# Layer 1's stack: the second feed-forward products issued together, and three score masks in one VectorE instruction

## The chip, the cores and the metric

The kernel runs on one core of a Trainium2 chip. A core has TensorE (PE in the profile; PEld is its weight load), VectorE (DVE), ScalarE (ACT), GpSimd (POOL) and SyncE (SP, which here issues DMAs). Times are device microseconds of one execution; lower is better.

## The reference

Four transformer-like layers are applied to an activation of 4 sequences x 1024 positions x 128 features, in fp32. Each layer has the same frame:

```python
h = _layernorm(x, axis=-1) * (1 + ca) + sa
x = x + ga * attn(h)
h = _layernorm(x, axis=-1) * (1 + cb) + sb
x = x + gb * ffn(h)
```

Layer 0's attention is a decaying linear attention and its feed-forward part a mixture of 8 experts. Layers 2 and 3 have chunked delta-rule attention and one expert chosen per sequence. Layer 1's attention is itself a stack of four blocks (`L = 4`, 16 heads of 8 features, feed-forward width 512), and this is where most of the change lies. One block is:

```python
q, k, v = x @ Wq + bq, x @ Wk + bk, x @ Wv + bv          # q, k through elu + 1
scores = q k^T within a chunk of 128 positions, lower triangle kept
out = (q KVcum + scores v) / (q . Kcum + sum of scores + eps)
x = _ln(x + out @ Wo + bo)
y = gelu(x @ W1 + b1) @ W2 + b2
x = _ln(x + y)
```

## The kernel before

Activations lie feature-major: 128 partitions hold the features, the free dimension holds 4 sequences x 1024 positions. One step `n` (of 8) takes a chunk of 128 positions of all four sequences, 512 columns, and a matmul result of 512 fp32 columns fills one of the eight PSUM banks.

Work within a half layer is written as Python generators ("chains") that ask for buffers (`take`, `one`), announce the time that the next instructions will take on each engine (`run`), and wait for marks (`wait`). `Flow.run` is a planner: it plays all chains against a clock of each engine, picks the chain of the lowest rank among those that can start within 0.1 us of the earliest, and so emits one fixed order of instructions. The order is then kept by the four compute engines (`in_order`). The announced lengths (`act_len`, `dve_len`, `mm_len` and numbers written out) thus never appear as instructions; they only decide what is issued ahead of what, in all four layers.

Layer 1's stack is `l1_attn`. Its chains, for 4 blocks x 8 steps:

- `prep_step` makes q, k and v. Each of q and k is a matmul into a `ps` bank, a DVE `min` into a buffer `fe` (L878) and an ACT relu (L879); ACT takes two exponentials (L888) and POOL adds them (L891). Then come the transposed keys (L903, L905), running sums of keys (L920, L923), denominators (L938, L939), and four masked copies of q (`qx`, L959).
- `scores` makes, for each sequence `b`, four score matrices at once with 32-row strips of the array, into the four banks of a "quad". There is one quad (`sp`). Its banks are written in the order 2, 3, 1, 0.
- `mask_dve` multiplies banks 0, 1, 2 by the triangle with three DVE instructions (L1010). `mask_act` copies bank 3 with ACT (L1023), and POOL masks the copy (L1026). When both are through, the quad is free.
- `values` multiplies the masked scores by v into the `acc` bank (L1085), after the carried state's share (L1071).
- `attn_out` divides, applies Wo and adds the residual (L1101, L1109).
- `tail_step`, run by two alternating chains, does the first norm, the feed-forward part (L1132 is the GELU, L1138 adds the result) and the second norm.

Banks are dealt out as follows: `ps` has three for all of `prep_step`, `state`, `attn_out` and `tail_step` and the norms, `acc` has one, the quad four. The feed-forward part before the change is

```python
po = yield from one("ps")
for f in range(4):
    u = yield from one("fu")
    pb = yield from one("ps")
    ...                                  # first product into pb, GELU into u, pb given back
    mm(po.t, W(1, "w2", 4 * l + f), flat(u.t), f == 0, f == 3)
    fl.give(u)
```

`norm` (used in all layers) transposes a step (L493), copies it out with ACT (L496), takes mean and variance with DVE (L502, L504), adds 1e-5 to the variance with DVE (L505, tile `ve`), raises to the power -0.5 with POOL (L507), scales with DVE (L510), transposes back (L518) and applies the affine part with ACT (L522 or L526). All matmuls go through the helper at L292, so the profile tells them apart by tiles.

Of the kernel before, what the change touches and what calls it, by code (L numbers as in the profile page):

```python
# [9 lines left out]
F32 = mybir.dt.float32  # L10
# [5 lines left out]
P = 128  # L16
# [218 lines left out]
def dve_len(n):  # L235
    return 0.16 + 0.00104 * n


def act_len(n):
    return 0.25 + 0.00083 * n  # L240
# [6 lines left out]
TR_LEN = 0.11  # L247


@with_exitstack  # L250
def adaln_stack_kernel(ctx: ExitStack, tc: tile.TileContext, a):
# [36 lines left out]
    def acc():  # L288
        return new(acp, [P, 512], "acc")
# [180 lines left out]
    def banks():  # L470
        return [ps() for _ in range(6)] + [acc() for _ in range(2)]
# [13 lines left out]
    def norm(fl, src, dst, affine):  # L485


        xb = yield from one("xt")
        pb = yield from one("ps")
        p = v4(pb.t)  # L490
        yield run(PE=4 * TR_LEN)
        for t in range(4):
            PE.transpose(p[:, t, :], src[:, t, :], ident)  # L493
        xt = xb.t
        yield run(ACT=act_len(512))
        S.copy(xt, p)  # L496
# [12 lines left out]
        for t in range(4):  # L509
            V.tensor_scalar(  # L510
                xt[:, t, :], xt[:, t, :], mv.t[:, t, 0:1], rs.t[:, t : t + 1], ALU.subtract, ALU.mult
            )
        fl.give(st, mv, ve, rs)
        pb = yield from one("ps")
        p = v4(pb.t)
        yield run(PE=4 * TR_LEN)
        for t in range(4):
            PE.transpose(p[:, t, :], xt[:, t, :], ident)  # L518
        fl.give(xb)
        if len(affine) == 1:  # L520
            yield run(ACT=act_len(512) + 0.1)
            S.activation(dst, p, AF.Identity, scale=affine[0][0], bias=affine[0][1])  # L522
        else:
            yield run(ACT=4 * act_len(P) + 0.4)
# [26 lines left out]
    def route(fl, n, wr, bias):  # L551


        rb, mb = (yield from one("rt")), (yield from one("rm"))
        p, oh1, oh2, rest = (rb.t[:, i, :].rearrange("p (b e) -> p b e", e=E) for i in range(4))
        m, r, s = (mb.t[:, i, :] for i in range(3))
        pb = yield from one("ps")
        lg = pb.t[:, : B * E].rearrange("p (b e) -> p b e", e=E)
        yield run(PE=4 * mm_len(E))
        for b in range(B):  # L560
            mm(lg[:, b, :], h4[:, b, n, :], wr)
        yield run(DVE=0.5)
        if bias is not None:
            V.tensor_tensor(p, lg, rep(bias, B), ALU.add)
            lg = p
        V.tensor_reduce(m, lg, AX.X, ALU.max)
        V.tensor_tensor(p if bias is None else rest, lg, spread(m, E), ALU.subtract)
        fl.give(pb)
        if bias is None:
            yield run("exp", ACT=0.3)  # L570
            S.activation(p, p, AF.Exp)
            yield run(DVE=0.6)
            normalise(p, s)
            yield run(DVE=2.0)
            first_max(p, m, oh1, r)
            V.scalar_tensor_tensor(rest, oh1, -BIG, p, ALU.mult, ALU.add)
            first_max(rest, m, oh2, r)
            V.tensor_tensor(oh1, oh1, oh2, ALU.add)
            V.tensor_tensor(p, p, oh1, ALU.mult)
        else:  # L580
            ex = yield from one("ex")
            yield run("exp", ACT=0.3)
            S.activation(ex.t, rest, AF.Exp)
            yield run(DVE=2.4)
            first_max(p, m, oh1, r)
            V.scalar_tensor_tensor(rest, oh1, -BIG, p, ALU.mult, ALU.add)
            first_max(rest, m, oh2, r)
            V.tensor_tensor(oh1, oh1, oh2, ALU.add)
            V.tensor_tensor(p, ex.t, oh1, ALU.mult)
            normalise(p, s)  # L590
            fl.give(ex)
        gt, gd = (yield from one("gt")), (yield from one("gd"))
        pb = yield from one("ps")
        yield run(PE=4 * TR_LEN)
        for b in range(B):
            PE.transpose(pb.t[:E, b * P : (b + 1) * P], p[:, b, :], ident)
        fl.give(rb, mb)
        yield run(ACT=act_len(512))
        S.copy(gt.t, pb.t[:E, :])
        fl.give(pb)  # L600
        yield run(SP=0.2)
        nc.sync.dma_start(gd.t, gt.t)
        fl.mark(("gates", n), 2.5)
        return gt, gd


    def l0():
# [113 lines left out]
        def attn():  # L721
            for n in range(NS):
# [8 lines left out]
                yield run(PE=(8 if n else 4) * mm_len(P + 1))  # L731
# [10 lines left out]
                yield run(ACT=4 * act_len(P))  # L742
# [16 lines left out]
                yield run(DVE=4 * dve_len(P))  # L759
# [32 lines left out]
        def experts(w, ways):  # L792
            for i in range(w, NS * L0J, ways):
# [28 lines left out]
                if k == L0J - 1:  # L822
                    yield run(DVE=4 * dve_len(P))
# [10 lines left out]
    def l1_attn():  # L834
        y4 = h4
        fl = flow()
        for kind, n in (("q", 3), ("k", 3), ("kt", 2), ("v", 2), ("rb", 2), ("fe", 2), ("tmp", 2), ("rde", 1),
                        ("at", 8), ("y1", 2), ("fu", 3)):
            stock(fl, kind, n)
        psum = banks()  # L840
        fl.stock("ps", psum[:3])
        fl.stock("acc", psum[3:4])
        fl.stock("sp", [psum[4:]])
# [24 lines left out]
        def prep_step(l, n):  # L868
# [3 lines left out]
            es = yield take("fe", 2)  # L872
            for e, o, nm in zip(es, (qb, kb), "qk"):
# [4 lines left out]
                V.tensor_scalar(flat(e.t), pb.t, C(f"l1_b{nm}{l}"), 0.0, ALU.add, ALU.min)  # L878
# [7 lines left out]
            yield run("exp", ACT=2 * act_len(512))  # L886
            for e in es:
                S.activation(e.t, e.t, AF.Exp)  # L888
            yield run(POOL=2 * pool_len(512))
            for e, o in zip(es, (qb, kb)):  # L890
                G.tensor_tensor(o.t, o.t, e.t, ALU.add)  # L891
            fl.give(*es)
# [11 lines left out]
            yield run(ACT=act_len(512))  # L904
# [12 lines left out]
            if n:  # L917
                yield run(DVE=4 * dve_len(P) + 0.15)
# [14 lines left out]
            yield run(PE=4 * mm_len(16))  # L933
# [17 lines left out]
            yield run(ACT=act_len(512))  # L951
# [5 lines left out]
            yield run(ACT=4 * act_len(512), POOL=4 * 0.45)  # L957
# [43 lines left out]
        def mask_dve():  # L1001
            for l, n in every:
                yield rank(l * NS + n)
                for b in range(B):
                    yield wait(("scores", l, n, b))
                    quad = ats[l, n, b][0]
                    at3 = yield take("at", 3)
                    yield run(DVE=3 * dve_len(512))
                    for d in range(3):
                        V.tensor_tensor(at3[d].t, v4(quad.t[d]), rep(mu, 4), ALU.mult)  # L1010
# [4 lines left out]
        def mask_act():  # L1015
            for l, n in every:
                yield rank(l * NS + n)
                for b in range(B):
                    yield wait(("scores", l, n, b))
                    quad = ats[l, n, b][0]  # L1020
                    a = yield from one("at")
                    yield run(ACT=act_len(512))
# [37 lines left out]
        def values():  # L1060
            for l, n in every:
# [13 lines left out]
                for b in range(B):  # L1075
# [3 lines left out]
                    at4 = at3 + [a]  # L1079
                    vz = ready[l, n][6].t  # L1080
                    yield run(PE=4 * mm_len(P) + 0.3)
                    for s in range(4):
                        for d in (3, 2, 1, 0):
                            g = slice(32 * d, 32 * d + 32)
                            PE.matmul(  # L1085
                                num[g, b, :], vz[:, b, s * P + 32 * d : s * P + 32 * d + 32], at4[d].t[:, s, :],
                                start=n == 0 and s == 0 and b == 0, stop=s == 3, skip_group_check=True,
                            )
                    fl.give(*at4)
# [31 lines left out]
        def tail_step(l, n, z):  # L1121
# [3 lines left out]
            po = yield from one("ps")  # L1125
            for f in range(4):
# [17 lines left out]
            if l == L1L - 1:  # L1144
                o = yield from one("y1")
                yield from norm(fl, yn, o.t, [(C("l1_gf"), C("l1_bef"))])
                yield run(DVE=4 * dve_len(P))
# [8 lines left out]
    def l1_ffn():  # L1156
# [39 lines left out]
        def experts(w, ways):  # L1196
            for i in range(w, NS * E, ways):
# [23 lines left out]
                if k == E - 1:  # L1221
                    yield run(DVE=4 * dve_len(P))
# [75 lines left out]
    def unit_keys(fl, src, kt, kf):  # L1298
# [5 lines left out]
        yield run(ACT=act_len(512))  # L1304
# [4 lines left out]
        yield run(DVE=4 * dve_len(P) + 7 * 0.16)  # L1309
# [9 lines left out]
        yield run(DVE=4 * dve_len(P))  # L1319
# [7 lines left out]
        yield run(ACT=act_len(512))  # L1327
# [3 lines left out]
    def add_gated(fl, i, n, val):  # L1331
        yield run(DVE=4 * dve_len(P))
        add_gated_step(i, n, val)
# [20 lines left out]
    def l2_l3():  # L1354
# [49 lines left out]
        def prep_step2(n, w):  # L1404
# [32 lines left out]
            def side():  # L1437
                if n:
                    yield run(DVE=0.15, ACT=4 * act_len(P))
# [72 lines left out]
        def out2():  # L1512
            for n in range(NS):
# [6 lines left out]
                yield run(PE=(8 if n else 4) * mm_len(P))  # L1520
# [4 lines left out]
                yield run(ACT=act_len(512))  # L1525
# [31 lines left out]
        def choose2():  # L1557
# [7 lines left out]
            yield run(PE=4 * mm_len(E))  # L1565
# [67 lines left out]
        def prep_step3(n, w):  # L1633
# [64 lines left out]
            yield run(ACT=act_len(512))  # L1698
# [8 lines left out]
            yield run(DVE=4 * dve_len(P))  # L1707
# [7 lines left out]
            def side():  # L1715
                yield run(ACT=4 * act_len(P))
# [36 lines left out]
        def state3():  # L1753
            for n in range(NS):
# [22 lines left out]
                if n < NS - 1:  # L1777
# [5 lines left out]
                    yield run(DVE=4 * dve_len(P))  # L1783
# [14 lines left out]
                if n < NS - 1:  # L1798
# [5 lines left out]
                    yield run(ACT=act_len(512))  # L1804
# [5 lines left out]
        def out3():  # L1810
            for n in range(NS):
# [7 lines left out]
                yield run(ACT=act_len(512))  # L1819
# [26 lines left out]
                yield run(PE=(8 if n else 4) * mm_len(P))  # L1846
# [30 lines left out]
        def choose3():  # L1877
# [13 lines left out]
            yield run(PE=4 * mm_len(E))  # L1891
# [169 lines left out]
```

## Time and profile before

| what | value |
|---|---|
| median of 3 runs | 2371.77 us (2369.8 to 2372.43) |
| the profiled execution | 2372.97 us; its span, first to last instruction, 2371.2 us |
| mean granted PE clock | 0.956 |
| PE busy | 2100.2 us, 89% of the span |
| DVE, ACT, POOL busy | 1336.7, 1135.5, 904.0 us |
| layer 1's stack, about | 395 to 1412 us of the span |
| PE busy in 420 to 1330 us | 847.26 of 910 us |

Rows of waits read "engine, tile and line that waited <- engine, tile and line that released it: us in total, times, longest". Rows of windows give the stretch, its length, then the busy time of each engine with its number of instructions. Rows of the timeline give start, length, engine, line, operation, output<-inputs, shape, count, and in brackets the idle time ahead and what ended it. One fp32 matmul appears as two passes (x2).

### The profile page before, as it was taken

Reading aid. Unit: us, or ns where it says so; the run is one execution under the profiler, and the core shown is the slowest. Engines: PE = TensorE matmul, PEld = TensorE weight load, DVE = VectorE, ACT = ScalarE, POOL = GpSimd, SP = SyncE. Lnnn points to the kernel's source line nnn. Section 1 sums busy time; section 2 is a strip of 40 time slices with the busy share of each in tenths; the row PEclk is TensorE's granted clock in tenths of the full one; section 3 lists DMA queues with packets and bytes.
Section 4 is the critical chain, followed back from the end, with each engine's and each line's share of the span. In section 5 each row is a group of like instructions: output and inputs, shape, how many; then the busy total and the mean of one; then the engine's idle time right before and its main releaser. Section 6 shows DMA issues by size and latency. Waiting matters only on the chain. (4 is left out here: it accounts for less than half of the span.)

```text
span 2371.2 us, 36944 instructions
## 1 busy us (share of the span) xinstructions
PE 2100.2 (89%) x13918; PEld 1323.4 (56%) x13918; DVE 1336.7 (56%) x4104; ACT 1135.5 (48%) x1957; POOL 904.0 (38%) x901
## 2 busy tenths in 40 slices
PE   5899997989999998999999859999799868898887
PEld 3665444655555555555555424444599734777763
DVE  5666334766667676666668644443676524464632
ACT  2554224555655555545555424444564426465634
POOL 0234444443434333443344213333554411636330
PEclk9999998999999999999999969999899989899998
DMA  6212320000000000000000003221000010000001
GB/s 232 77 59 85 99 75 1 2 1 1 1 1 2 1 1 1 1 1 1 1 2 1 1 5 103 72 71 36 1 1 1 1 36 0 1 1 1 1 1 53
DMA packets 29010, 61.46 MB, mean 26 GB/s; under 512 B 4256, under 2 KB 4512, under 8 KB 27808
## 3 DMA queue, kind: packets, MB, share of 16 engines
q1 hardware_dynamic: 27072, 53.86, 7.1%
q0 software_dynamic: 896, 3.16, 0.4%
q8 instruction: 109, 1.79, 0.3%
q10 hardware_dynamic: 864, 2.09, 0.2%
q14 instruction: 69, 0.57, 0.1%
HBM read 56.74 MB, written 2.36 MB: 25 GB/s over the span
## 5 line engine op out<-in xcount | busy, mean ns | idle before, releaser
L292 PE MATMUL ps<-h,w 128*128 128x512 f32 x826 | 414.9, 614 | 24.4 <-DMA w<-in_g,offi 14.6
L507 POOL TENSOR_TENSOR rs<-ve,mhalf 128x4 f32<-128x4 f32 x136 | 140.1, 1031 | 430.6 <-DVE ve L505 418.9
L1026 POOL TENSOR_TENSOR at<-at,cst 128x512 f32<-128x512 f32 x128 | 163.3, 1276 | 278.3 <-ACT at L1023 274.2
L292 PEld LDWEIGHTS ps<-h,w 128*128 128x128 f32 x826 | 151.8, 196 | 185.6 <-issue 145.0
L292 PE MATMUL acc<-fu,w 128*128 128x512 f32 x464 | 222.6, 596 | 1.1 <-POOL fu L810 0.9
L1010 DVE TENSOR_TENSOR at<-ps,cst 128x512 f32<-128x512 f32 x256 | 164.0, 682 | 95.8 <-PE acc L292 77.1
L1242 POOL TENSOR_TENSOR lv<-cl,cst 128x512 f32<-128x512 f32 x112 | 141.2, 1273 | 146.4 <-PE ps L292 54.8
L292 PE MATMUL ps<-fu,w 128*128 128x512 f32 x320 | 175.8, 635 | 13.3 <-ACT fu L1132 11.6
L292 PE MATMUL acc<-qx,k 32*128 32x512 f32 (+1 forms) x768 | 177.5, 514 | 10.2 <-DVE at L1010 8.6
L810 POOL TENSOR_TENSOR fu<-fu,gate 128x512 f32<-128x512 f32 x88 | 111.1, 1270 | 128.5 <-DVE fu L806 107.5
L292 PE MATMUL ps<-y,w 128*128 128x512 f32 x256 | 144.9, 649 | 12.5 <-ACT y L522 4.9
L1209 ACT ACTIVATE fu<-ps,cols 128x512 f32<-128x512 f32 x128 | 87.9, 688 | 131.0 <-PE ps L292 128.1
L292 PE MATMUL ps<-qx,k 32*128 32x512 f32 x512 | 146.2, 647 | 0.0
L1085 PE MATMUL ps<-at,vz 128*32 128x128 f32 x4096 | 140.9, 277 | 3.4 <-DVE at L1010 3.4
L1023 ACT COPY at<-acc 128x512 f32<-128x512 f32 x128 | 74.9, 585 | 140.4 <-PE acc L292 114.4
L292 PEld LDWEIGHTS acc<-fu,w 128*128 128x128 f32 x464 | 85.4, 190 | 100.5 <-issue 83.7
L1213 POOL TENSOR_TENSOR fu<-fu,gate 128x512 f32<-128x512 f32 x64 | 82.7, 1296 | 151.3 <-ACT fu L1209 136.9
L1085 PEld LDWEIGHTS ps<-at,vz 128*32 128x32 f32 x4096 | 105.7, 110 | 58.5 <-issue 33.6
L1132 ACT ACTIVATE fu<-ps,cols 128x512 f32<-128x512 f32 x128 | 87.8, 686 | 83.6 <-PE ps L292 82.5
L292 PEld LDWEIGHTS acc<-qx,k 32*128 32x128 f32 x768 | 68.4, 186 | 59.9 <-issue 33.8
L806 DVE TENSOR_TENSOR fu<-fu,ps 128x512 f32<-128x512 f32 x76 | 51.4, 685 | 82.0 <-PE ps L292 75.6
L526 ACT ACTIVATE h<-ps,mod 128x128 f32<-128x128 f32 x176 | 66.1, 462 | 63.4 <-PE ps L518 63.4
(481 smaller groups left out, 4447.3 us busy)
## 6 DMA issues: line engine op xcount, KB each, us to landing
gate<-gd SPq DMA_DIRECT2D x96, 256.0 KB
w<-in_w SPq DMA_DIRECT2D x7, 1024.0 KB
gate<-gd SPq DMA_DIRECT2D x16, 224.0 KB
gate<-gd SPq DMA_DIRECT2D x16, 192.0 KB
gate<-gd SPq DMA_DIRECT2D x16, 160.0 KB
x<-in_x SPq DMA_DIRECT2D x8, 256.0 KB
gate<-gd SPq DMA_DIRECT2D x16, 128.0 KB
out_x<-x SPq DMA_DIRECT2D x8, 256.0 KB
```

What stands on the lines that cost most here:

```text
L292: PE.matmul(out, lhsT, rhs, start=start, stop=stop)
L507: G.tensor_tensor(rs.t, ve.t, mhalf, ALU.pow)
L526: S.activation(dst[:, t, :], p[:, t, :], AF.Identity, scale=affine[t][0], bias=affine[t][1])
L810: G.tensor_tensor(u.t, u.t, g.t, ALU.mult)
L1010: V.tensor_tensor(at3[d].t, v4(quad.t[d]), rep(mu, 4), ALU.mult)
L1023: S.copy(a.t, v4(quad.t[3]))
L1026: G.tensor_tensor(a.t, a.t, rep(mu, 4), ALU.mult)
L1085: PE.matmul(num[g, b, :], vz[:, b, s * P + 32 * d : s * P + 32 * d + 32], at4[d].t[:, s, :], start=n == 0 and s == 0 and b == 0, stop=s == ...
L1132: S.activation(flat(u.t), pb.t, AF.Gelu, bias=C(f"l1_b1{l}", f))
L1209: S.activation(u.t, pa.t, AF.Relu, bias=C("l1f_b1", 2 * e + j))
L1213: G.tensor_tensor(us[1].t, us[1].t, g.t, ALU.mult)
L1242: G.tensor_tensor(b.t, cl.t, rep(lvl[:, k * P : (k + 1) * P], B), ALU.mult)
```

## The change

In layer 1's stack:

1. `tail_step` makes the four first products and GELUs first, keeping the four `u`, and only then takes a bank `po` and issues the four second products. `fu` grows from 3 to 5 buffers.
2. Three of the eight banks become one tensor `wide`; the quad of `scores` is its three slices and one `acc` bank. `mask_dve` masks all three with one instruction into a buffer `a3` of three times the width; the stock of eight `at` buffers becomes two `a3` and two `a1`.
3. The two `fe` buffers become one of double width, with one exponential over both.

In `norm` of all layers, the addition of 1e-5 moves from DVE to POOL. Many lengths announced to the planner are changed in all layers; the lines that only do this are cut below save for examples. All other layers use the three slices of `wide` as three banks.

```diff
 def act_len(n):
-    return 0.25 + 0.00083 * n
+    return 0.26 + 0.00084 * n
...
+COPY_LEN = 0.59
+STT_LEN = 0.345
...
-    psp = ctx.enter_context(tc.tile_pool(name="psum", bufs=6, space=bass.MemoryType.PSUM))
+    psp = ctx.enter_context(tc.tile_pool(name="psum", bufs=3, space=bass.MemoryType.PSUM))
     acp = ctx.enter_context(tc.tile_pool(name="pacc", bufs=2, space=bass.MemoryType.PSUM))
+    wide = ctx.enter_context(tc.tile_pool(name="pwide", bufs=1, space=bass.MemoryType.PSUM)).tile(
+        [P, 3 * 512], F32, tag="wide", name="wide"
+    )
...
     def banks():
-        return [ps() for _ in range(6)] + [acc() for _ in range(2)]
+        return [ps() for _ in range(3)] + [acc() for _ in range(2)] + [wide[:, 512 * i : 512 * i + 512] for i in range(3)]
...
-        yield run(ACT=act_len(512))
+        yield run(ACT=COPY_LEN)
         S.copy(xt, p)
...
-        yield run(DVE=4 * dve_len(P) + 5 * 0.16)
+        yield run(DVE=1.74)
...
-        V.tensor_scalar(ve.t, mv.t[:, :, 1], 1e-5, None, ALU.add)
-        yield run(POOL=1.0)
+        yield run(POOL=1.3)
+        G.tensor_scalar(ve.t, mv.t[:, :, 1], 1e-5, None, ALU.add)
         G.tensor_tensor(rs.t, ve.t, mhalf, ALU.pow)
-        yield run(DVE=4 * dve_len(P))
+        yield run(DVE=4 * STT_LEN)
...
-        for kind, n in (("q", 3), ("k", 3), ("kt", 2), ("v", 2), ("rb", 2), ("fe", 2), ("tmp", 2), ("rde", 1),
-                        ("at", 8), ("y1", 2), ("fu", 3)):
+        for kind, n in (("q", 3), ("k", 3), ("kt", 2), ("v", 2), ("rb", 2), ("tmp", 2), ("rde", 1), ("a1", 2),
+                        ("y1", 2), ("fu", 5)):
             stock(fl, kind, n)
+        stock(fl, "fe", 1, (P, 2, B, P))
+        stock(fl, "a3", 2, (P, 3, B, P))
...
-        fl.stock("sp", [psum[4:]])
+        fl.stock("sp", [psum[5:] + psum[4:5]])
...
-            yield run("exp", ACT=2 * act_len(512))
-            for e in es:
-                S.activation(e.t, e.t, AF.Exp)
+            yield run("exp", ACT=1.1)
+            both = eb.t.rearrange("p i b t -> p (i b t)")
+            S.activation(both, both, AF.Exp)
...
-                    at3 = yield take("at", 3)
-                    yield run(DVE=3 * dve_len(512))
-                    for d in range(3):
-                        V.tensor_tensor(at3[d].t, v4(quad.t[d]), rep(mu, 4), ALU.mult)
+                    at3 = yield from one("a3")
+                    yield run(DVE=dve_len(3 * 512))
+                    V.tensor_tensor(
+                        at3.t.rearrange("p d s q -> p (d s) q"), wide.rearrange("p (s q) -> p s q", q=P), rep(mu, 12), ALU.mult
+                    )
...
-                    yield run(PE=4 * mm_len(P) + 0.3)
+                    yield run(PE=0.93)
...
-            po = yield from one("ps")
+            us = []
             for f in range(4):
                 u = yield from one("fu")
                 pb = yield from one("ps")
...
                 fl.give(pb)
+                us.append(u)
+            po = yield from one("ps")
+            for f in range(4):
                 yield run(PE=mm_len(512))
-                mm(po.t, W(1, "w2", 4 * l + f), flat(u.t), f == 0, f == 3)
-                fl.give(u)
+                mm(po.t, W(1, "w2", 4 * l + f), flat(us[f].t), f == 0, f == 3)
+                fl.give(us[f])
```

More of the change, by code (lines that the diff above doesn't have):

```diff
@@ L520, in norm @@
         if len(affine) == 1:
-            yield run(ACT=act_len(512) + 0.1)
+            yield run(ACT=0.78)
             S.activation(dst, p, AF.Identity, scale=affine[0][0], bias=affine[0][1])
         else:
-            yield run(ACT=4 * act_len(P) + 0.4)
+            yield run(ACT=2.28)
             for t in range(4):
@@ L558, in route @@
         lg = pb.t[:, : B * E].rearrange("p (b e) -> p b e", e=E)
-        yield run(PE=4 * mm_len(E))
+        yield run(PE=0.8)
         for b in range(B):
@@ L597, in route @@
         fl.give(rb, mb)
-        yield run(ACT=act_len(512))
+        yield run(ACT=COPY_LEN)
         S.copy(gt.t, pb.t[:E, :])
@@ L730, in attn @@
                 pbs = yield take("ps", 2)
-                yield run(PE=(8 if n else 4) * mm_len(P + 1))
+                yield run(PE=(1.79 if n else 0.9))
                 for b in range(B):
@@ L741, in attn @@
                     V.reciprocal(rd.t, rd.t)
-                yield run(ACT=4 * act_len(P))
+                yield run(ACT=4 * 0.39)
                 for b in range(B):
@@ L758, in attn @@
                 fl.give(o)
-                yield run(DVE=4 * dve_len(P))
+                yield run(DVE=4 * STT_LEN)
                 add_gated_step(0, n, v4(pb.t))
@@ L822, in experts @@
                 if k == L0J - 1:
-                    yield run(DVE=4 * dve_len(P))
+                    yield run(DVE=4 * STT_LEN)
                     for b in range(B):
@@ L871, in prep_step @@
             qb, kb = (yield from one("q")), (yield from one("k"))
-            es = yield take("fe", 2)
+            eb = yield from one("fe")
+            es = [eb.t[:, i] for i in range(2)]
             for e, o, nm in zip(es, (qb, kb), "qk"):
@@ L877, in prep_step @@
                 yield run(DVE=dve_len(512), ACT=act_len(512))
-                V.tensor_scalar(flat(e.t), pb.t, C(f"l1_b{nm}{l}"), 0.0, ALU.add, ALU.min)
+                V.tensor_scalar(flat(e), pb.t, C(f"l1_b{nm}{l}"), 0.0, ALU.add, ALU.min)
                 S.activation(flat(o.t), pb.t, AF.Relu, bias=C(f"l1_b{nm}{l}"))
@@ L885, in prep_step @@
                 mm(v4(vp.t)[:, b, :], y4[:, b, n, :], W(1, "wv", l))
-            yield run("exp", ACT=2 * act_len(512))
-            for e in es:
-                S.activation(e.t, e.t, AF.Exp)
+            yield run("exp", ACT=1.1)
+            both = eb.t.rearrange("p i b t -> p (i b t)")
+            S.activation(both, both, AF.Exp)
             yield run(POOL=2 * pool_len(512))
             for e, o in zip(es, (qb, kb)):
-                G.tensor_tensor(o.t, o.t, e.t, ALU.add)
-            fl.give(*es)
+                G.tensor_tensor(o.t, o.t, e, ALU.add)
+            fl.give(eb)
             q, k = qb.t, kb.t
@@ L903, in prep_step @@
                 PE.transpose(v4(kp.t)[:, b, :], k[:, b, :], ident)
-            yield run(ACT=act_len(512))
+            yield run(ACT=COPY_LEN)
             S.copy(kt.t, v4(kp.t))
@@ L917, in prep_step @@
             if n:
-                yield run(DVE=4 * dve_len(P) + 0.15)
+                yield run(DVE=4 * STT_LEN + 0.15)
                 for b in range(B):
@@ L932, in prep_step @@
             den = db.t[:, : B * 16].rearrange("p (a b) -> p a b", a=B)
-            yield run(PE=4 * mm_len(16))
+            yield run(PE=0.8)
             for b in range(B):
@@ L950, in prep_step @@
             fl.give(rde)
-            yield run(ACT=act_len(512))
+            yield run(ACT=COPY_LEN)
             S.copy(rb.t, v4(rp.t))
@@ L956, in prep_step @@
             qx, vz = (yield from one("qx")), (yield from one("vz"))
-            yield run(ACT=4 * act_len(512), POOL=4 * 0.45)
+            yield run(ACT=4 * 0.72, POOL=4 * 0.3)
             for s in range(4):
@@ L1020, in mask_act @@
                     quad = ats[l, n, b][0]
-                    a = yield from one("at")
-                    yield run(ACT=act_len(512))
+                    a = yield from one("a1")
+                    yield run(ACT=COPY_LEN)
                     S.copy(a.t, v4(quad.t[3]))
@@ L1078, in values @@
                     _, at3, a = ats.pop((l, n, b))
-                    at4 = at3 + [a]
+                    at4 = [at3.t[:, d] for d in range(3)] + [a.t]
                     vz = ready[l, n][6].t
-                    yield run(PE=4 * mm_len(P) + 0.3)
+                    yield run(PE=0.93)
                     for s in range(4):
@@ L1085, in values @@
                             PE.matmul(
-                                num[g, b, :], vz[:, b, s * P + 32 * d : s * P + 32 * d + 32], at4[d].t[:, s, :],
+                                num[g, b, :], vz[:, b, s * P + 32 * d : s * P + 32 * d + 32], at4[d][:, s, :],
                                 start=n == 0 and s == 0 and b == 0, stop=s == 3, skip_group_check=True,
                             )
-                    fl.give(*at4)
+                    fl.give(at3, a)
                 nums[l, n] = nb
@@ L1146, in tail_step @@
                 yield from norm(fl, yn, o.t, [(C("l1_gf"), C("l1_bef"))])
-                yield run(DVE=4 * dve_len(P))
+                yield run(DVE=4 * STT_LEN)
                 add_gated_step(1, n, o.t)
@@ L1221, in experts @@
                 if k == E - 1:
-                    yield run(DVE=4 * dve_len(P))
+                    yield run(DVE=4 * STT_LEN)
                     for b in range(B):
@@ L1303, in unit_keys @@
             PE.transpose(v4(pb.t)[:, b, :], src[:, b, :], ident)
-        yield run(ACT=act_len(512))
+        yield run(ACT=COPY_LEN)
         S.copy(kt, v4(pb.t))
@@ L1308, in unit_keys @@
         ns, rn = (yield from one("ns")), (yield from one("rn"))
-        yield run(DVE=4 * dve_len(P) + 7 * 0.16)
+        yield run(DVE=2.14)
         for b in range(B):
@@ L1318, in unit_keys @@
         G.tensor_tensor(rn.t, ns.t, mhalf, ALU.pow)
-        yield run(DVE=4 * dve_len(P))
+        yield run(DVE=4 * STT_LEN)
         for b in range(B):
@@ L1326, in unit_keys @@
             PE.transpose(v4(pb.t)[:, b, :], kt[:, b, :], ident)
-        yield run(ACT=act_len(512))
+        yield run(ACT=COPY_LEN)
         S.copy(kf, v4(pb.t))
@@ L1331, in add_gated @@
     def add_gated(fl, i, n, val):
-        yield run(DVE=4 * dve_len(P))
+        yield run(DVE=4 * STT_LEN)
         add_gated_step(i, n, val)
@@ L1438, in side @@
                 if n:
-                    yield run(DVE=0.15, ACT=4 * act_len(P))
+                    yield run(DVE=0.2, ACT=4 * 0.39)
                     V.tensor_scalar(bd.t, be.t, de_col, None, ALU.mult)
@@ L1519, in out2 @@
                 pb = yield from one("ps")
-                yield run(PE=(8 if n else 4) * mm_len(P))
+                yield run(PE=(1.79 if n else 0.9))
                 for b in range(B):
@@ L1524, in out2 @@
                         mm(v4(pb.t)[:, b, :], s.t[:, b, :], kde.t[:, b, :], False, True)
-                yield run(ACT=act_len(512))
+                yield run(ACT=COPY_LEN)
                 S.copy(o.t, v4(pb.t))
@@ L1564, in choose2 @@
             V.tensor_scalar(mean, mean, 1.0 / T, None, ALU.mult)
-            yield run(PE=4 * mm_len(E))
+            yield run(PE=0.8)
             p = pb.t[:, : B * E].rearrange("p (b e) -> p b e", e=E)
@@ L1697, in prep_step3 @@
                 PE.transpose(v4(pb.t)[:, b, :], up.t[:, b, :], ident)
-            yield run(ACT=act_len(512))
+            yield run(ACT=COPY_LEN)
             S.copy(lo.t, v4(pb.t))
@@ L1706, in prep_step3 @@
                 mm(gm[:, b, :], kf.t[:, b, :], kf.t[:, b, :])
-            yield run(DVE=4 * dve_len(P))
+            yield run(DVE=4 * STT_LEN)
             for b in range(B):
@@ L1715, in side @@
             def side():
-                yield run(ACT=4 * act_len(P))
+                yield run(ACT=4 * 0.39)
                 for b in range(B):
@@ L1782, in state3 @@
                         mm(v4(pb.t)[:, b, :], kdw.t[:, b, :], un.t[:, b, :])
-                    yield run(DVE=4 * dve_len(P))
+                    yield run(DVE=4 * STT_LEN)
                     if n:
@@ L1803, in state3 @@
                         PE.transpose(v4(pb.t)[:, b, :], r.t[:, b, :], ident)
-                    yield run(ACT=act_len(512))
+                    yield run(ACT=COPY_LEN)
                     S.copy(s.t, v4(pb.t))
@@ L1818, in out3 @@
                     PE.transpose(v4(pb.t)[:, b, :], un.t[:, b, :], ident)
-                yield run(ACT=act_len(512))
+                yield run(ACT=COPY_LEN)
                 S.copy(ut.t, v4(pb.t))
@@ L1845, in out3 @@
                 pb = yield from one("ps")
-                yield run(PE=(8 if n else 4) * mm_len(P))
+                yield run(PE=(1.79 if n else 0.9))
                 for b in range(B):
@@ L1890, in choose3 @@
             pb = yield from one("ps")
-            yield run(PE=4 * mm_len(E))
+            yield run(PE=0.8)
             p = pb.t[:, : B * E].rearrange("p (b e) -> p b e", e=E)
```

## The prediction

> **What bounds the kernel now.** I read the page first (busy shares, and the row of granted clocks), then stage windows, then the list of what TensorE (PE) waited for in layer 1's stack, then the groups and the timeline there. PE is the busiest engine of the kernel, and of layer 1's stack more than of the rest:
>
> ```profile
> PE 2100.2 (89%) x13918; PEld 1323.4 (56%) x13918; DVE 1336.7 (56%) x4104; ACT 1135.5 (48%) x1957; POOL 904.0 (38%) x901
> ```
> ```profile
> core 0: us, PE busy (x) PEld busy (x) DVE busy (x) ACT busy (x) POOL busy (x), PEclk, DMA share, GB/s
> 0.00:395.00 395.00, 343.30 (x1248) 194.54 (x1249) 199.24 (x727) 151.62 (x284) 146.50 (x125) 0.97 0.29 94
> 395.00:1412.00 1017.00, 921.76 (x8161) 540.04 (x8159) 670.58 (x1860) 523.93 (x803) 398.42 (x452) 0.97 0.01 1
> 1412.00:1720.00 308.00, 285.01 (x907) 144.65 (x907) 143.49 (x481) 134.54 (x249) 118.79 (x95) 0.95 0.18 56
> 1720.00:2371.20 651.20, 550.11 (x3607) 444.15 (x3605) 323.37 (x1036) 325.41 (x621) 240.34 (x230) 0.93 0.03 9
> ```
>
> Layer 1's stack is the second row, 1017 us of 2371. PE is idle there for 1017 - 922 = 95 us, and only that (with small gaps that pipelined matmuls hide) can be won: the change takes no matmul away. In its steady part, 420 to 1330 us, PE idles 910 - 847 = 63 us. The waits of PE there, of which these rows matter (total, times, longest):
>
> ```profile
> PE acc L292 <- DVE at L1010: 7.8, 16, 0.9
> PE ps L292 <- ACT q L879: 6.5, 6, 2.3
> PE ps L292 <- ACT fu L1132: 5.8, 10, 1.2
> ...
> PE ps L1085 <- DVE at L1010: 3.4, 3, 1.5
> ...
> PE ps L292 <- ACT k L879: 2.7, 5, 1.1
> ...
> PE ps L903 <- ACT k L879: 2.4, 2, 1.2
> ...
> PE ps L949 <- ACT fu L1132: 1.8, 2, 0.9
> ```
>
> Three kinds are in it. Rows ending in `DVE at L1010` are PE waiting for the masks, 7.8 + 3.4 = 11.2 us. Rows ending in `ACT q` or `ACT k` are mostly matmuls that want a bank which ACT still reads, not data: 6.5 + 2.7 + 2.4 and 1.4 of smaller rows, 13.0 us. Rows ending in `ACT fu` are PE waiting for a GELU, 7.6 us. The bank waits fit the code: `ps` has three banks in this stage, and `tail_step` takes one (`po`) before its first matmul and keeps it over four GELUs. Those are far apart (787.7, 793.7, 799.1, 804.5 us in one tail), so `po` is held over 20 us of a step of some 29 us (910 us for about 31 steps), and the rest of the stage lives on two banks.
>
> **The change, part by part** (own time of the profiled execution: 2372.97, span 2371.2 and 1.8 around it; the median of the three runs is 2371.77, 1.2 lower).
>
> *Second products together, `po` late.* The bank is then held for four products, 4 x 0.86 = 3.4 us (a pair of passes starts 0.86 apart in the timeline), and the DVE add of 0.75: near 5 us instead of over 20. Three banks rotate for most of the step. Of the 13.0 us of bank waits I take 10. The GELU waits, 7.6 us, go for the first three products, since their `u` is old by then; I take 6. Where these stalls go: next late are the transposes' data (`ACT kt`, 5.5 us in the same list) and the norms, so not all is won. `fu` grows from 3 to 5 because four are held at once; a second tail finds one left, but the GELUs of two tails do not overlap in the trace.
>
> At the stage's end nothing else fills PE, and a tail is a chain:
>
> ```profile
> 1339.64 1.12 PE L292 MATMUL ps<-y,w 128*128 128x512 f32 x2 [0.93 <-ACT y L522]
> 1341.55 1.13 PE L292 MATMUL ps<-fu,w 128*128 128x512 f32 x2 [0.78 <-ACT fu L1132]
> ...
> 1345.71 1.02 PE L292 MATMUL ps<-y,w 128*128 128x512 f32 x2
> 1347.57 1.12 PE L292 MATMUL ps<-fu,w 128*128 128x512 f32 x2 [0.84 <-ACT fu L1132]
> ```
>
> First product, GELU, second product, in turn: from 1339.64 to the add at 1352.10, 12.5 us. Regrouped, four firsts and four seconds run back to back, 8 x 0.86 = 6.9, with the GELUs beneath: about 5 us less. Three such tails run in a row (1339, 1358, 1375); the first has filler, so I count somewhat under two: 8 us.
>
> *One mask for three banks.* The row L1010 is 682 ns for 512 columns; a column costs 1.05 ns by the rows L920 and L1138, one operation at 128 columns (343 ns) and at 512 (747). So 1536 columns cost about 0.68 + 1024 x 0.00105 = 1.76 us against 1.96 to 2.05 for three (1.28 for two and 0.68 in the timeline). 0.2 to 0.3 us less, 128 times, is 27 to 38 us of DVE, which is 66% busy and bounds nothing. On the path are the 19 mask waits: 19 x 0.25 = 5 us. Here the Trainium skill speaks against the edit: Perfetto Trace Analysis, Optimizing Scalar/DVE Operations, says that where such an engine is not saturated but makes bubbles elsewhere, breaking instructions up can finish work sooner. By that rule the fusion costs up to 1.76 - 0.68 = 1.08 us in 19 waits, +20 us. But `scores` writes bank 2 first and bank 0 last, while the masks run 0, 1, 2: the first mask already starts after the last matmul and the next scores already wait for the last mask. Nothing overlapped, so I take the row: -5.
>
> *The variance's epsilon moves from DVE to POOL* (136 norms, all layers). Row L505 has a median of 170 ns and a longest of 1235; POOL's row for the power is 1018. On POOL the addition is unmeasured. Below, nothing: it stands next to the power, no engine is crossed more often, and DVE no longer holds it. Above, 0.30, POOL's copy of 128 columns (L962, 298 ns). The skill's rule (GPSIMD Engine Reference, Engine selection) is against: elementwise work belongs on VectorE, about twice as slow here for two inputs, roughly line rate for one; twice 0.17 would be 0.34. By the rule's price +0.17 x 136 = +23 us if every norm lay on the path; by the row's ends, -0.17 to +0.13 on each. PE hides nearly all of them in the steady stages; some 25 are serial (stage ends, routers): I take +2. What queues behind POOL's longer turn is the key masks (L1026), with 270 us of idle before them.
>
> *One exponential of 1024 columns for two of 512* saves ACT 0.1 us 32 times; the q half reaches POOL at most 0.6 later, which POOL's idle time covers (52 us before L891). Nothing; uncovered, +0.6 x 32 = 19. *Wider tiles for masks and exponentials, split stocks:* the same two quads in flight, no cost. *Other layers' banks* are now partly slices of one tensor: no cost, since `h` and `x`, too, are single tensors that several engines use in slices without waiting for each other. No DMA is moved.
>
> *New costs in the planner* (`COPY_LEN`, `STT_LEN` and others) emit nothing but reorder every stage. The trace before can't show that order. I take zero and bound it by a third of PE's idle time outside layer 1, (52 + 23 + 101) / 3 = 59, halved since stages err independently: +-30.
>
> Sum: -10 - 6 - 8 - 5 + 2 = -27. 2373 - 27 = 2346 on the profiled execution, 2345 against the median.
>
> **The rivals.** *The burst (slower).* Today each second product is a loose 0.86 us filler. Bundled, they hold PE for 3.4 us; a scores round due inside waits up to 2.6 us, 1.3 in the mean. For it: a round of scores, mask and restart is 1.3 + 2.0 + 0.2 = 3.5 us, four of them nearly half a step, and there is one quad. Against: each product is its own planned step, so others may slip between. If one round in each of 32 steps is hit, +42, minus the 27: +15, 2387. It decides from 0.85 us lost per step on (27 / 32).
>
> *PE was full anyway (no change).* Around 764 to 812 us the PE rows stand back to back, with under 3 us of waits; a stall removed reappears at the next `ACT kt`. Then only the stage's end remains, and the new order may eat it: 2368.
>
> *The two-bank corset was the whole story (much faster).* The planner itself could not place matmuls for want of banks, so gaps too short for the wait list go as well. Half of the 95 idle us and the 8 at the end: 2315.
>
> That the banks are not really freed is excluded by the diff: `po` is taken after the loop.
>
> **How the numbers follow.** Forecast 0.50 at 2345 (its own range 2325 to 2365); burst or a bad new order 0.28 at 2387; no change 0.12 at 2368; much faster 0.10 at 2315. About 0.2% (5 us) is what a measurement can tell from no change here. Faster: 0.48 + 0.10 + 0.03 = 0.61; same 0.08; slower 0.31. The range leaves out the better half of the fast rival and the worse third of the slow one: 2310 to 2393.
>
> **What would show it.** Right: between 395 and 1412 us the stage is some 25 us shorter with PE busy time unchanged; rows `ACT q`, `ACT k`, `ACT fu` fall below 10 us together; the mask row reads 128x1536 near 1.76 us; the last tails take about 8 us from first product to add. Wrong: mask waits of PE grow, products `ps<-fu,w` stand four in a row with scores late behind them, a POOL row for `ve` of over 0.5 us, or stages 0, 2 and 3 move by more than the stack does.

## The result and the profile after

The changed kernel takes 2430.74 us (median of 4 runs, 2429.13 to 2437.61) against 2372.10 for the kernel before (4 runs): a ratio of 1.0254, 95% interval 1.0233 to 1.0275. It is slower by 59 us; 2345 was forecast. The profiled execution took 2437.61 us with a span of 2435.8. The page after, busy times and granted clock:

```profile
PE 2126.6 (87%) x13918; PEld 1328.9 (55%) x13918; DVE 1290.0 (53%) x3712; ACT 1120.7 (46%) x1918; POOL 939.9 (39%) x1037
...
PEclk9999998999999999999999789999999979899998
```

The same 13918 matmuls, DVE 47 us less busy, and yet 65 us more of span. Where it went shows only by stage. Windows of the kernel after, cut at the stages' own ends: layer 0, layer 1's stack, layer 1's feed-forward part, layers 2 and 3. The first number after the length is PE's busy time, with its count of matmuls; the one after POOL's is the granted clock.

```profile
10.00:402.00 392.00, 340.85 (x1204) 184.34 (x1204) 182.93 (x664) 140.80 (x264) 140.81 (x129) 0.99 0.28 88
402.00:1384.40 982.40, 915.83 (x8168) 539.60 (x8168) 633.90 (x1520) 507.79 (x766) 424.25 (x534) 0.97 0.01 1
1384.40:1678.50 294.10, 265.28 (x710) 120.03 (x711) 116.41 (x377) 113.37 (x190) 97.88 (x85) 0.94 0.18 58
1678.50:2435.80 757.30, 604.68 (x3838) 484.89 (x3836) 356.46 (x1150) 357.03 (x695) 276.64 (x285) 0.91 0.02 8
```

The stack, which the change was about, is 40 us shorter: 982 against 1022. (By its own lines it ran from 369.0 to 1391.1 us before; the 395 to 1412 us given ahead of the result lie 26 and 21 us late.) The three stages that were meant to be left alone lost 33, 14 and 57 us. The waits of PE in layer 0 of the kernel after name the new tensor:

```profile
PE wide L297 <- POOL fu L815: 6.3, 10, 2.2
PE wide L297 <- ACT fu L809: 5.8, 9, 0.8
...
PE wide L297 <- DVE fu L811: 3.8, 4, 0.9
PE wide L297 <- ACT h L531: 2.6, 2, 1.7
PE wide L297 <- ACT kd L683: 2.5, 4, 0.9
PE wide L297 <- DVE x L830: 1.7, 2, 1.2
```

These are waits of matmuls that write `wide`. Of their kinds the same stage before had only the first, `POOL fu`, with 0.9 us. The long rows of other banks stood there before as well (17.0, 9.8 and 4.3 us now; 17.6, 10.6 and 5.5 then). So three of eight banks carry the new waits of this stage.

All stages of all kernels, in us. The stack is measured from the first to the last instruction of its own lines; the feed-forward part (FF) ends where the code of layers 2 and 3 begins. "Ratio" is that of the runs to those of the kernel before on the same chip, with its 95% interval; on the chips of e1 to e13 that kernel's median lay between 2370.5 and 2373.1. The stages are those of the one profiled execution.

| kernel | median | ratio | layer 0 | stack | FF | layers 2, 3 |
|---|---|---|---|---|---|---|
| before | 2372.10 | | 369.0 | 1022.1 | 280.0 | 700.1 |
| after | 2430.74 | 1.0254 (1.0233 to 1.0275) | 402.0 | 982.4 | 294.1 | 757.3 |
| e1_split | 2322.71 | 0.9784 (0.9767 to 0.9800) | 362.1 | 983.1 | 280.8 | 694.4 |
| e2_wide_only | 2483.93 | 1.0467 (1.0449 to 1.0484) | 407.3 | 1020.9 | 294.8 | 758.7 |
| e3_split_ve_dve | 2337.66 | 0.9851 (0.9835 to 0.9868) | 364.9 | 990.1 | 280.8 | 699.6 |
| e4_prices_only | 2378.18 | 1.0022 (1.0015 to 1.0028) | 363.7 | 1026.0 | 280.7 | 701.5 |
| e5_ve_pool_only | 2370.68 | 0.9993 (0.9984 to 1.0002) | 367.7 | 1046.8 | 280.3 | 678.8 |
| e6_late_po_only | 2349.80 | 0.9905 (0.9889 to 0.9922) | 369.3 | 996.5 | 279.9 | 702.0 |
| e7_split_early_po | 2376.97 | 1.0022 (1.0013 to 1.0030) | 363.0 | 1035.1 | 280.7 | 696.9 |
| e8_split_three_masks | 2330.05 | 0.9825 (0.9808 to 0.9841) | 361.2 | 988.6 | 280.6 | 695.7 |
| e9_grouped_bank_early | 2395.58 | 1.0093 (1.0074 to 1.0113) | 363.9 | 1045.8 | 280.7 | 703.0 |
| e10_old_lengths | 2337.13 | 0.9862 (0.9844 to 0.9881) | 366.6 | 988.7 | 291.9 | 685.0 |
| e11_late_po_ve_pool | 2301.17 | 0.9701 (0.9682 to 0.9720) | 368.1 | 973.5 | 280.4 | 677.5 |
| e13_late_ve_fused | 2332.08 | 0.9831 (0.9815 to 0.9847) | 367.2 | 999.9 | 280.4 | 677.7 |

### The profile page after: what moved, and what is told of

It reads as the page before. It is cut to its first block, busy times and chain, and to the rows that moved or that the text cites. A ratio compares the mean times of both kernels' runs of the same rounds, so it can differ in the third digit from the quotient of the medians.

```text
span 2435.8 us, 36568 instructions
## 1 busy us (share of the span) xinstructions
PE 2126.6 (87%) x13918; PEld 1328.9 (55%) x13918; DVE 1290.0 (53%) x3712; ACT 1120.7 (46%) x1918; POOL 939.9 (39%) x1037
## 5 line engine op out<-in xcount | busy, mean ns | idle before, releaser
L1017 DVE TENSOR_TENSOR a<-wide,cst 128x1536 f32<-128x1536 f32 x128 | 224.2, 1751 | 127.4 <-PE acc L297 112.9
L1035 POOL TENSOR_TENSOR a<-a,cst 128x512 f32<-128x512 f32 x128 | 163.7, 1279 | 271.5 <-ACT a L1032 271.3
L297 PE MATMUL ps<-h,w 128*128 128x512 f32 x478 | 254.2, 626 | 14.5 <-DMA w<-in_g,offi 8.0
L297 PE MATMUL wide<-fu,w 128*128 128x512 f32 x468 | 230.8, 606 | 25.8 <-POOL fu L815 6.3
L297 PE MATMUL acc<-qx,k 32*128 32x1 f32 (+1 forms) x512 | 177.0, 447 | 0.6 <-ACT a L1032 0.6
L297 PE MATMUL wide<-qx,k 32*128 32x512 f32 x768 | 147.5, 646 | 7.6 <-DVE a L1017 7.2
L1094 PE MATMUL acc<-a,vz 128*32 128x128 f32 x4096 | 141.6, 277 | 5.8 <-DVE a L1017 5.3
L1094 PEld LDWEIGHTS acc<-a,vz 128*32 128x32 f32 x4096 | 105.5, 110 | 73.8 <-issue 50.5
L297 PE MATMUL acc<-h,w 128*128 128x512 f32 x236 | 120.9, 602 | 0.0
L297 PE MATMUL wide<-h,w 128*128 128x512 f32 (+1 forms) x200 | 105.7, 612 | 14.5 <-DMA w<-in_g,offi 7.1
```

The lines of the kernel that those rows point to most:

```text
L297: PE.matmul(out, lhsT, rhs, start=start, stop=stop)
L1017: V.tensor_tensor(at3.t.rearrange("p d s q -> p (d s) q"), wide.rearrange("p (s q) -> p s q", q=P), rep(mu, 12), ALU.mult)
L1035: G.tensor_tensor(a.t, a.t, rep(mu, 4), ALU.mult)
L1094: PE.matmul(num[g, b, :], vz[:, b, s * P + 32 * d : s * P + 32 * d + 32], at4[d][:, s, :], start=n == 0 and s == 0 and b == 0, stop=s == 3 ...
```

## The experiments

**The three slices as one tensor, e1 and e2.** Outside the stack, e1 gives each of the three banks its own tensor, with every engine's order of instructions kept. e2 does the opposite to the kernel before: outside the stack, three of its banks become slices of one tensor.

```diff
-        return [ps() for _ in range(3)] + [acc() for _ in range(2)] + [wide[:, 512 * i : 512 * i + 512] for i in range(3)]
+        return [ps() for _ in range(3)] + [acc() for _ in range(2)] + third
...
+            if half is l1_attn:          # e2: "is not"
+                wide = pw.tile([P, 3 * 512], F32, tag="wide", name=f"wide{i}")
+                third = [wide[:, 512 * j : 512 * j + 512] for j in range(3)]
+            else:
+                third = [pw.tile([P, 512], F32, tag=f"third{j}", name=f"third{i}_{j}") for j in range(3)]
```

> The kernel after, with the same order of instructions, but the three slices are one tensor in layer 1's stack alone; in layers 0, 2, 3 and in layer 1's feed-forward part they are three tensors of one bank each. Theory A (in those stages each access to one slice is ordered behind the accesses to the other two slices, since they are one tensor): the stages outside the stack, which lost 33 + 15 + 57 = 105 us, win most of it back, 2330 to 2350 us. Theory B (the new announced lengths and the moved epsilon spoil the order): same as the kernel after, 2425 to 2435.

> The kernel before, with its own lengths and its epsilon on DVE; only, outside layer 1's stack, three of the eight banks are slices of one tensor. Theory A: slower than before by most of the 105 us, 2450 to 2480. Theory B: as before, 2365 to 2380.

e1 took 2322.71, 108 us less than the kernel after; e2 2483.93, 112 us more than the kernel before. That is 7 and 4 us beyond the spans of theory A. Both ways the loss lies in the three stages outside the stack (40 + 13 + 63 in e1, 38 + 15 + 59 in e2), while the stack moves by 1. So the tensor alone makes the loss, whatever the order and the lengths. In e1's layer 0 three rows of PE's waits still name one of the three banks (`third`), 2.2 us together:

```profile
PE third L295 <- POOL fu L813: 1.1, 2, 0.9
...
PE third L295 <- ACT h L529: 0.7, 1, 0.7
PE third L295 <- DVE va L680: 0.4, 1, 0.4
```

What a matmul is made to wait for stands in the compiled programs. Here are two second products of layer 0's experts, with the engines whose semaphores they wait for, first in the kernel after and then in e1 (`wide` holds both the sum and other chains' results):

```
after:  matmul wide  <- fu0, w      waits ACT, POOL
        matmul wide  <- fu2, w      waits ACT, POOL
e1:     matmul third2 <- fu0, w     waits POOL
        matmul third2 <- fu2, w     waits POOL
```

POOL is the data, the gated `u`. ACT has no part in this sum: it was reading another slice. Of the 87 such products of layer 0 that write these banks, 20 wait for ACT in the kernel after and none in e1. It works the other way too: where two SiLUs read two slices one after the other, the first waits in the kernel after for the matmul that in e1 only the second waits for. The slices do not overlap, but the accesses to one PSUM tensor were ordered as if they did.

Not every wait on these banks comes from that. In layers 2 and 3, PE's waits for `wide` sum to 81.5 us in the kernel after, and those for the same banks as three tensors still to 52.8 us in e1.

PE is also busy longer with the same matmuls. In layers 2 and 3 of the kernel after it is 604.68 us at a granted clock of 0.91. e1's rows for layer 0 and for layers 2 and 3:

```profile
10.00:362.10 352.10, 327.09 (x1204) 184.74 (x1204) 182.44 (x660) 140.56 (x264) 141.00 (x130) 0.99 0.30 98
...
1626.00:2320.40 694.40, 580.36 (x3838) 469.93 (x3836) 364.06 (x1150) 358.32 (x695) 277.19 (x285) 0.94 0.03 9
```

In layers 2 and 3 that is 24 us of the 63. The clock cannot be all of it: in layer 0 the busy time also grew by 14 us (340.85 against 327.09) with the clock at 0.99 in both. How much belongs to the clock was not separated. That gaps lower it was not tested either; the Trainium skill (TensorE: Matmul & The Clock Gate, Part 1) says that PE falls to half its clock after an idle window of about 3.4 us.

**The announced lengths alone, e4.** The new `run(...)` lengths in the kernel before, wherever the instruction is the same in both; no instruction changed.

```diff
-        yield run(ACT=act_len(512))
+        yield run(ACT=COPY_LEN)
...
-                    yield run(PE=4 * mm_len(P) + 0.3)
+                    yield run(PE=0.93)
```

> The kernel before with the lengths announced to the planner as after, nothing else changed. Theory A: 2360 to 2385, a change of order with no fixed sign. Theory B: 2420 to 2480, since the order alone would make the loss outside the stack.

2378.18, +0.22%: the new order alone costs about 5 us here, not 59. Theory B falls.

**The epsilon, e3 and e5.** e3 is e1 with it back on DVE; e5 is the kernel before with it on POOL. In both the lengths announced for this step change too.

```diff
-        yield run(POOL=1.3)
-        G.tensor_scalar(ve.t, mv.t[:, :, 1], 1e-5, None, ALU.add)
+        V.tensor_scalar(ve.t, mv.t[:, :, 1], 1e-5, None, ALU.add)
+        yield run(POOL=1.0)
```

> As the first kernel of this call, with the epsilon of the norms back on DVE. Theory A: within 10 us of the first kernel. If the move to POOL costs (theory C): 15 to 30 us faster than the first.

> The kernel before with the epsilon of the norms on POOL and the two lengths of that step as announced after. Theory D (DVE was held at this little instruction, and POOL takes it for nearly nothing; it is worth the 15 us that separate e1 and e3): 2355 to 2365. The prediction's step (+2, a little slower): 2373 to 2378.

e3 is 15 us slower than e1, which neither theory had: C falls, and the move gains there. e5 as a whole does not move (interval 0.9984 to 1.0002), between what theory D and the prediction gave it; by stage it gains 21 us in layers 2 and 3 and loses 25 in the stack. The instruction itself, in the stretch from 420 to 1310 us (shortest, median, longest ns), on DVE in e3 and on POOL in e1:

```profile
L508 DVE TENSOR_SCALAR ve<-mv x67: 169/170/1243, 422.5 to 1308.2; 128x4 f32<-128x4 f32 x67
```
```profile
L509 POOL TENSOR_SCALAR ve<-mv x68: 219/229/242, 419.9 to 1309.3; 128x4 f32<-128x4 f32 x68
```

Its cost on POOL, 229 ns, lies within the prediction's ends. Its longest on DVE is seven times its median; on POOL it never strays. The longest one of this stretch in e3, below what POOL did at that time:

```profile
561.29 1.27 POOL L1033 TENSOR_TENSOR a<-a,cst 128x512 f32<-128x512 f32 x1 [3.30 <-ACT a L1030]
```
```profile
561.34 1.24 DVE L508 TENSOR_SCALAR ve<-mv 128x4 f32<-128x4 f32 x1
```

The addition starts just behind POOL's instruction and ends just behind it. So it is with all 16 of e3's 136 additions that took over 0.3 us: each began while POOL ran an instruction, and each ended 23 to 30 ns after one of POOL's had ended.

**The late bank, e6 and e7.** e6 puts the new feed-forward part alone (with five buffers `fu` for three) into the kernel before; e7 takes it out of e1.

```diff
-            po = yield from one("ps")
+            us = []
...
+                us.append(u)
+            po = yield from one("ps")
+            for f in range(4):
                 yield run(PE=mm_len(512))
-                mm(po.t, W(1, "w2", 4 * l + f), flat(u.t), f == 0, f == 3)
+                mm(po.t, W(1, "w2", 4 * l + f), flat(us[f].t), f == 0, f == 3)
```

> The kernel before with the second products together and their bank taken late (fu 5), nothing else. If this carries the stack's gain of some 40 us: 2330 to 2345. The prediction's sum gave it 24: 2349. If PE was full anyway: 2370.

> e1 with the feed-forward part as before (bank taken early, fu 3), the one mask and all else kept. If the late bank carries the stack's gain: 2350 to 2365, 24 to 40 slower than e1's 2323. If the one mask carries it: within 10 of e1.

e6 took 2349.80, 21 us less; its stack alone is 26 shorter (997 against 1022). The prediction's sum gave it 2349. e7 is 54 us slower than e1, 12 beyond what was expected, and even slower than the kernel before, although it has every other part of the change: with two rotating banks the rest is worth nothing in total.

**Products together, bank still early, e9.** Of the two things that the edit does, this keeps one.

```diff
             us = []
+            po = yield from one("ps")
             for f in range(4):
...
-            po = yield from one("ps")
             for f in range(4):
```

> e1 with the second products together, but their bank taken ahead of the first product, as before. Theory E (it is the bank, held over the GELUs, that costs): as e7, 2365 to 2380. Theory F (it is the GELU waits between the products): as e1, 2320 to 2330.

2395.58, 73 us slower than e1, 63 of them in the stack: F falls, and E holds with more loss than it gave (2380 at most). Where in the stack it lies shows when the stage is cut at the end of the last score product:

| kernel | second products | bank taken | to the last scores, us | from there to the end, us |
|---|---|---|---|---|
| before | one by one | early | 961.1 | 61.1 |
| e7_split_early_po | one by one | early | 971.5 | 63.6 |
| e9_grouped_bank_early | together | early | 1000.1 | 45.8 |
| e1_split | together | late | 936.7 | 46.4 |
| e6_late_po_only | together | late | 954.1 | 42.4 |

All 63 us that e9 loses against e1 lie ahead of the last scores: there the held bank is what cost, and the grouping gains nothing. At the end it is the other way round: grouped products shorten it with either bank. Part of that is less work, since the kernel before has four additions of the feed-forward part left after its last scores and e1, e6 and e9 have three.

Progress shows in how many matmul passes start in the same 890 us of the stack. First the kernel before, then e1, e7 and e9; the first figure after the length is PE's busy time, with its count:

```profile
420.00:1310.00 890.00, 829.10 (x7599) 489.56 (x7596) 599.68 (x1589) 471.92 (x715) 364.56 (x411) 0.98 0.01 1
```
```profile
420.00:1310.00 890.00, 849.38 (x7794) 499.79 (x7794) 584.25 (x1351) 468.56 (x700) 391.88 (x491) 0.98 0.01 1
```
```profile
420.00:1310.00 890.00, 817.75 (x7506) 481.88 (x7506) 563.26 (x1266) 471.17 (x686) 379.01 (x476) 0.99 0.01 1
```
```profile
420.00:1310.00 890.00, 815.95 (x7234) 475.68 (x7234) 556.79 (x1237) 439.25 (x655) 364.59 (x460) 0.96 0.00 1
```

In the same time e1 starts 7794, e9 7234. Grouping did not end the waits for GELUs either; e1, then e9:

```profile
PE ps L295 <- ACT fu L1139: 2.0, 5, 0.4
```
```profile
PE ps L295 <- ACT fu L1140: 5.2, 7, 1.4
```

**One mask or three, e8 and e13.** e8 is e1 with three mask instructions on three tensors; e13 is e11 with the single mask.

```diff
-                    yield run(DVE=dve_len(3 * 512))
-                    V.tensor_tensor(at3.t.rearrange(...), wide.rearrange(...), rep(mu, 12), ALU.mult)
+                    yield run(DVE=3 * dve_len(512))
+                    for d in range(3):
+                        V.tensor_tensor(at3.t[:, d], v4(quad.t[d]), rep(mu, 4), ALU.mult)
```

> e1 with three mask instructions over three banks that are three tensors in the stack too; buffers as in e1. The prediction's step (0.25 us at 19 waits): 2328, 5 slower than e1. If the fused mask matters more than its waits show: 2335 to 2350. If breaking up is better, as the skill's rule says: 2303 to 2318.

> e11 with the three masks in one instruction over three banks that are one tensor in the stack alone. By the prediction's step (5 us of waits): 2290 to 2300. If a single edit's effect in the stack is mostly the planner's new order: anywhere in 2285 to 2320, with the stages outside the stack unchanged within 3 us of e11's.

e8 is 7 us slower than e1 (10 by the ratios), about the 5 that were counted. But PE does not wait longer for its masks in e8 (11.1 us in 420 to 1310 us, e1 11.6); what rose there is the wait for GELUs (11.0 against 2.0). And e13 is 31 us slower than e11, all in the stack, and 12 beyond the widest of its expectations. The sign is not settled: e13 also splits the mask buffers into two kinds, and the planner's order changes with every length. PE's waits for masks did fall in e13; what rose are waits for ACT's work on k and on the GELUs. e11's and e13's rows (those of `ACT q` and `ACT k` sum to 2.4 us in e11):

```profile
PE acc L292 <- DVE at L1010: 6.7, 11, 0.7
```
```profile
PE ps L293 <- ACT k L881: 7.6, 8, 1.1
PE ps L293 <- ACT fu L1135: 5.8, 10, 1.3
...
PE wide L293 <- DVE a L1011: 5.2, 12, 0.6
```

**The lengths of before in e1, and the best version, e10 and e11.** e10 reverses e4's edit on e1. e11 is the kernel before with two edits, the late bank (diff of e6) and the epsilon on POOL (that of e5).

> e1's instructions with the lengths announced before. If the new lengths are worth something to the stack: 2330 to 2345. If they are noise in the order, either side of 2323 by up to 20; stages 2 and 3 then should read about 679 us as in e5, which has the same lengths and the same norm, 15 less than e1.

> The kernel before with the late bank and with the epsilon on POOL. If the epsilon's move pays once three banks rotate: 2330 to 2340, 10 to 20 under e6's 2350 with the stack near 985. If e5's moves between stages were only order: the stack anywhere within 25 of e6's 997, stages 2 and 3 near 679.

e10 is 14 us slower than e1, within both spans expected: by stage 9 won in layers 2 and 3 (685, not the 679 expected), 21 lost elsewhere. It announces 1.81 us for the norm's statistics where e5 and e11 announce 1.74; nothing else differs in layer 1's feed-forward part but the names of the banks, and e13 has e10's names. Yet PE's order in that part differs from e11's in e10 and is e11's own in e13, and it takes 292 us in e10, 280 in e11 and e13. e11, at 2301.17, is the fastest of all: 3.0% under the kernel before (interval 2.8 to 3.2), and 29 us faster than the best that was expected of it.

## Why the prediction was wrong

- **Other layers' banks: the step that failed.** "No cost, since `h` and `x`, too, are single tensors that several engines use in slices without waiting for each other." The runs put 108 us (after to e1) and 112 us (before to e2) in its place. The argument went from SBUF tensors to a PSUM tensor, for which no row of the trace before spoke; so the step had no price and no rival, and the range's top was 38 us too low. Whether other ways of slicing a PSUM tensor avoid the waits was not run. The prediction named the sign that came true: the other stages moved by more (104 us) than the stack did (40).
- **The bank held over the GELUs** was right in mechanism. The rows of `ACT q`, `ACT k` and `ACT fu`, 20.6 us before, fell to 7.4 in the kernel after, as forecast (below 10). Its rows for these and for the masks, 420 to 1330 us:

```profile
PE wide L297 <- DVE a L1017: 7.0, 15, 0.6
...
PE acc L1094 <- DVE a L1017: 5.3, 5, 2.2
PE ps L297 <- ACT k L887: 4.0, 6, 1.9
...
PE ps L297 <- ACT fu L1141: 2.3, 5, 0.7
...
PE ps L297 <- ACT q L887: 1.1, 4, 0.3
```

  The size depends on the company. 16 us in the steady part and 8 at the end were counted. Alone (e6) the edit won 26 in the stack, near the 24, but 7 ahead of the last scores and 19 behind: the sum was met by luck. It is 52 in e1's company (e7), 73 between e5 and e11. Nor does grouping take away the GELU waits credited to it (6 us): with the bank early, in e9, the rows of `ACT fu` sum to 7.6 us in 420 to 1310 us, as before, and to 2.0 in e1. The mis-sized term is the bank in company: the wait list showed 13 us of it. The likely reason is that a planner that lacks banks spreads the matmuls out rather than let them queue; no run isolates it.
- **The stage's end.** From the last scores to the end of the stack it was 61 us before and is 46 after: 15 won where 8 were counted, with one feed-forward part less left to do. A last tail still takes 12 us from its first product (1362.11) to its add (1374.2), not 8; the last tails overlap instead.
- **The mask's length** was right: 1.76 us forecast, and the page after has

```profile
L1017 DVE TENSOR_TENSOR a<-wide,cst 128x1536 f32<-128x1536 f32 x128 | 224.2, 1751 | 127.4 <-PE acc L297 112.9
```

  1751 ns. Its worth of 5 us is not shown. The waits for masks that it was to shorten went from 11.2 to 12.3 us (the two mask rows above), so e8's 7 us meets the 5 by luck, and e13 is 31 us the other way. The skill's rule on breaking instructions up, weighed there, stays undecided. (The saving of DVE time, from 1.96 to 2.05 down to 1.76, is 26 to 37 us by its own numbers, not 27 to 38; nothing hangs on it.)
- **The epsilon** was put at +2. It is -15 in e3 against e1, -49 in e11 against e6, and nothing in e5 against before. Layers 2 and 3 gain in all three pairs (5, 25 and 21 us); the stack gains 7 and 23 in two and loses 25 in e5. The step priced the addition on DVE at its median and left out the long ones, though the row of before showed them (longest 1235 ns). How much of the gain they are and how much is the new order was not separated. 229 ns is 1.35 times the 170 of DVE, not the twice that was weighed.
- **The planner's order** was bounded by 30 us either way; e4 moved 5. As a bound that was fair for a sum, but not by stage: in e5 one stage lost 25 us and another gained 21.
- **The burst**, the rival on the slower side, did not happen: the stack became shorter. The products (two passes each) stand one at a time with others between them, as in this tail of the kernel after:

```profile
654.21 1.02 PE L297 MATMUL ps<-fu,w 128*128 128x512 f32 x2
...
655.93 1.02 PE L297 MATMUL ps<-fu,w 128*128 128x512 f32 x2
...
656.79 1.02 PE L297 MATMUL ps<-y,w 128*128 128x512 f32 x2
...
657.65 1.02 PE L297 MATMUL ps<-fu,w 128*128 128x512 f32 x2
...
658.94 1.02 PE L297 MATMUL ps<-fu,w 128*128 128x512 f32 x2
```

  The kernel was slower, to which the prediction gave 0.31, for a reason that no rival held.

## What to carry to other kernels

Check what else is carried by an edit that only "renames" storage: buffers that were separate and become slices of one tensor may be ordered against each other (here 108 to 112 us), and the place to look is the stages that the change is not about. When a buffer is scarce, count how long each holder keeps it, not only the waits that the profile shows; take it as late as the code allows, and try the other edits again after that. With a planner that orders everything, the effect of one edit is known only by several pairs of kernels with and without it; here one edit, the epsilon's, moved the stack by +25 us in one pair and by -23 in another.

## What was not expected of the hardware

The small addition for the norms costs DVE 170 ns in the median but up to 1243 ns in the steady part, and in e3 each one over 0.3 us began while POOL was busy and ended within 30 ns of the end of a POOL instruction. On POOL it is steady at 219 to 242 ns. So the engine that is slower at it by the median was no worse a place for it in any of the three pairs that tried it, and better in two. Why DVE is held behind POOL here no run shows.
